# A post-norm decoder layer: V's weight fold moved beside the first unit's scores, projection biases on VectorE, first transposes of the feed-forward moved into the last gate

## The chip, the core and the metric

The kernel runs on one core of one Trainium2 chip. The metric is the device time in microseconds (us), the median of several executions. Everything is float32. The engines are TensorE (PE, with its weight loads PEld), VectorE (DVE), ScalarE (ACT), GpSimd (POOL) and SyncE (SP), which here only issues transfers. Each engine works through its own instructions in order.

## The reference, cut to what matters

```python
# x: (4, 1024, 512); every product in float32
q = (x @ wq_w + wq_b) @ vq_w.T + vq_b      # likewise k, v
# 32 channels of 16: q, k, v -> (32, 4, 1024, 16)
attn = softmax(q @ k.T / 4); o = attn @ v  # o is then reshaped and mixed
x = layernorm(x + o @ wo_w.T + wo_b)
# gated step: a convolution of two taps along the features, 4 gates
it, ot, gt, ft = split(ctx + conv(x) + bias)
ct = sigmoid(ft) * z0c + sigmoid(it) * tanh(gt); ht = sigmoid(ot) * tanh(ct)
x = layernorm(x + concat(ht, ct))
# feed-forward: x rounded to integers and scaled back, ternary weights
x = layernorm(x + dequantised(x) @ (ternary - 1).T + bias)
```

## The kernel before, in words

Two linear layers in a row are one, so the kernel first folds each pair of weights into one: `fold` (L269 to 279) multiplies `w_n` with `v_t` into `w_q`, `w_k` and `w_v`, 16 matmuls for each, in PSUM tiles that DVE and ACT copy out. The folded bias of q and k is `foldc` (L289 to 299, 16 narrow matmuls each), that of v is `foldb` (L283 to 286, 4 matmuls). SP loads the weights in the order of use; the first transfer of all is `b_o` (L60), which the output projection needs much later.

Then come 32 units of attention, a unit being 4 of the 32 channels of one batch element. `project` (L330) makes q and k of two units in pieces of 160 or 176 tokens; ACT adds the bias into `packed`, and SP scatters its rows over quadrants of 32 partitions (`to_quadrants`, L318; the tiles are named `qk`). `nat` (L390) makes the scores with queries on the partitions; DVE reduces them to the row maxima (L407), which go back into a spare row of q through DRAM (`shift`). `scores` (L444) makes the scores the other way round, ACT exponentiates them, and `weigh` (L477) multiplies with v. The loop over units (L563) starts at u = -1: this stage has only the `nat` of unit 0, 16 steps of two pairs of matmuls, and between them the pieces of `fill`: unit 2's q and the 16 pieces of `project_v` (L348), which make v of batch element 0 and which DVE evacuates, adding `b_v` (L356). From u = 0 on, the stages hold all kinds of work. Two PSUM rings are used: `ps_nat` has two tiles of two banks, `ps_st` four tiles of one bank. The order of instructions in this part, and in the tail, is the one in which the Python code issues them (`manual_schedule`).

The tail has steps: `after(n, work)` (L667) puts work n steps later, `step()` (L670) closes a step and issues what is due. A step is one gate, or one tile of the projection or of the feed-forward. For each pair of batch elements, (0, 2) and then (1, 3), there are 32 gates (`gate`, L719: three taps of 4 matmuls, two DVE additions, one ACT activation). After the fourth gate of a block `combine` (L738) forms the cell on POOL and, a step later, `second` (L745) takes the tanh on ACT. `second_norm` (L759) normalises and quantises the first two tiles ahead. Then `feed_forward` (L834) runs 16 tiles of 128 tokens. A tile is `turn` (L788: 4 transposes on TensorE, one ACT copy to `xq_t`), `feed` (L796: 4 matmuls into a ring of two PSUM tiles), `quantise` of a later tile (L779: ACT, then DVE L784 and L785), `ff_bias` (L828) and `residual` (L802: DVE L804 adds the PSUM tile, L805 takes statistics). `third_norm` (L807) normalises finished tiles and stores them, spread over later steps: aggregates on DVE (L95), a square root on ACT (L102), a reciprocal (L103) and the scaling (L111) on DVE. Between the two feed-forwards lie 16 tiles of `project_out`, whose residual input is loaded by `load_residual` a given number of steps into the first one.

Of the kernel before, what the change touches and what calls it, by code (L numbers as in the profile page):

```python
# [51 lines left out]
class Handed:  # L52
# [3 lines left out]
    def __init__(self, tc, a, shared, attn_d, eps):  # L56
        self.eps = eps
        self.nc, self.a, self.shared, self.attn_d = tc.nc, a, shared, attn_d
        self.b_o = shared.tile([P, D], F32, tag="b_o", name="b_o")
        self.nc.sync.dma_start(self.b_o, a["wo_b"].partition_broadcast(P))  # L60
        self.big, self.y, self.stats = {}, {}, {}
# [8 lines left out]
    def load_w_o(self):  # L70
        self.w_o = self.shared.tile([P, FT, D], F32, tag="w_v", name="w_o")
        self.nc.sync.dma_start(self.w_o, self.a["wo_wT"].rearrange("(t p) f -> p t f", p=P))
# [19 lines left out]
    def means(self, stats, pool, name, t0=0, n=NT):  # L92
        mv = pool.tile([P, NT, 2], F32, tag="mv", name=f"mv{name}_{t0}")
        for t in range(t0, t0 + n):
            self.nc.vector.bn_aggr(mv[:, t, :], stats[:, t, :])  # L95
        return mv

    def deviations(self, mv, pool, name, t0=0, n=NT):

        nc = self.nc  # L100
        rstd = pool.tile([P, NT], F32, tag="rstd", name=f"rstd{name}_{t0}")
        nc.scalar.activation(rstd[:, t0 : t0 + n], mv[:, t0 : t0 + n, 1], AF.Sqrt, bias=self.eps, scale=1.0)  # L102
        nc.vector.reciprocal(rstd[:, t0 : t0 + n], rstd[:, t0 : t0 + n])  # L103
        return rstd
# [87 lines left out]
def attention(ctx, tc, a, attn_d, ident, shared, hand):  # L192
# [52 lines left out]


    with tc.tile_pool(name="setup", bufs=2) as sp, tc.tile_pool(
        name="setup_ps", bufs=2, space=PSUM
    ) as ps:
        xts = {}  # L250
        for which, (w, v, dst) in enumerate((("wq", "vq", w_q), ("wk", "vk", w_k), ("wv", "vv", w_v))):
            w_n = sp.tile([P, FT, D], F32, tag="w_n", name=f"w_n{which}")
            v_t = sp.tile([P, FT, D], F32, tag="v_t", name=f"v_t{which}")
            for m in range(FT):
                rows = slice(m * P, (m + 1) * P)
                nc.sync.dma_start(w_n[:, m, :], a[f"{w}_w"][rows, :])
                nc.sync.dma_start(v_t[:, m, :], a[f"{v}_wT"][rows, :])
            w_b = sp.tile([P, FT], F32, tag="w_b", name=f"w_b{which}")
            nc.sync.dma_start(w_b, a[f"{w}_b"])
            if which < 2:  # L260
                v_b = sp.tile([P, FT], F32, tag="v_bc", name=f"v_b{which}")
                nc.sync.dma_start(v_b, a[f"{v}_bc"])
            else:
                v_b = sp.tile([P, D], F32, tag="v_b", name=f"v_b{which}")
                nc.sync.dma_start(v_b, a[f"{v}_b"].partition_broadcast(P))
            if which == 1:
                xts[0] = load_x(0)

            pts = [ps.tile([P, D], F32, tag="ps", bufs=6, name=f"fold{which}_{f}") for f in range(FT)]  # L269
            for m in range(FT):  # L270
                for f in range(FT):
                    nc.tensor.matmul(  # L272
                        pts[f], w_n[:, m, f * P : (f + 1) * P], v_t[:, m, :], start=m == 0, stop=m == FT - 1
                    )
            for f in range(FT):
                if f % 2:
                    nc.scalar.copy(dst[:, f, :], pts[f])
                else:
                    nc.vector.tensor_copy(dst[:, f, :], pts[f])
            w_bb = sp.tile([P, FT, P], F32, tag="w_bb", name=f"w_bb{which}")  # L280
            nc.vector.tensor_copy(w_bb, w_b.unsqueeze(2).to_broadcast([P, FT, P]))
            if which == 2:
                pb = ps.tile([P, D], F32, tag="ps", bufs=6, name=f"foldb{which}")  # L283
                for m in range(FT):
                    nc.tensor.matmul(pb, w_bb[:, m, :], v_t[:, m, :], start=m == 0, stop=m == FT - 1)
                nc.vector.tensor_add(b_v, pb, v_b)  # L286
                continue

            pc = ps.tile([P, FT, 32], F32, tag="pc", name=f"foldc{which}")  # L289
            for f in range(FT):  # L290
                for m in range(FT):
                    nc.tensor.matmul(
                        pc[:, f, :],
                        v_t[:, m, f * P : (f + 1) * P],
                        w_bb[:, m, 0:32],
                        start=m == 0,
                        stop=m == FT - 1,
                    )
            nc.vector.tensor_add((b_q, b_k)[which], pc[:, :, 0], v_b)

    small = ctx.enter_context(tc.tile_pool(name="asmall", bufs=2))
    packs = ctx.enter_context(tc.tile_pool(name="packs", bufs=1))
    atp = ctx.enter_context(tc.tile_pool(name="at", bufs=14))
    obuf = ctx.enter_context(tc.tile_pool(name="obuf", bufs=2))
    onp = ctx.enter_context(tc.tile_pool(name="onp", bufs=1))
    dpool = ctx.enter_context(tc.tile_pool(name="rec_d", bufs=2, space=bass.MemoryType.DRAM))
    ps_nat = ctx.enter_context(tc.tile_pool(name="ps_nat", bufs=2, space=PSUM))
    ps_st = ctx.enter_context(tc.tile_pool(name="ps_st", bufs=4, space=PSUM))
    ctx.enter_context(tc.manual_schedule())
# [20 lines left out]
    def project(p, which, t0, n, packed):  # L330

        b, gg = divmod(p, 4)
        w, bias = ((w_q, b_q), (w_k, b_k))[which]
        cols = slice(t0, t0 + n)
        pt = ps_st.tile([P, QW], F32, tag="st", name=f"proj{p}_{which}_{t0}")
        for f in range(FT):
            nc.tensor.matmul(  # L337
                pt[:, 0:n], w[:, f, gg * P : (gg + 1) * P], xts[b][:, f, cols], start=f == 0, stop=f == FT - 1
            )
        nc.scalar.activation(packed[:, cols], pt[:, 0:n], AF.Identity, bias=bias[:, gg : gg + 1], scale=1.0)  # L340
        if t0 + n == S:
            to_quadrants(2 * p, which, packed)
            if which == 0 and p > 0:
                late_rows.append(lambda: to_quadrants(2 * p + 1, 0, packed))
            else:
                to_quadrants(2 * p + 1, which, packed)

# [42 lines left out]
    def nat(u, i, pair):  # L390
# [4 lines left out]
        pt = ps_nat.tile([P, 2, 512], F32, tag="nat", name=f"nat{u}_{i}_{pair}")  # L395
        for n in range(2):
            r = 32 * (2 * pair + n)
            nc.tensor.matmul(  # L398
                pt[:, n, :],
                q_ts[u % 4][r : r + 32, qt * P : (qt + 1) * P],  # L400
                k_ts[u % 4][r : r + 32, kh * 512 : kh * 512 + 512],
                start=True,
                stop=True,
            )

        def reduce():
            nc.vector.tensor_reduce(  # L407
                mxs[u][:, qt, 2 * pair : 2 * pair + 2, kh], pt, AX.X, ALU.max, negate=True
            )
# [150 lines left out]
    for piece in qk_pieces(0, 0) + qk_pieces(0, 1):  # L560
        piece()

    for u in range(-1, NU):  # L563
# [5 lines left out]
        if u == -1:  # L569
            fill += [piece for t in range(NT) for piece in v_pieces(0, t)]  # L570
        elif units[u][0] + 1 < B:
            fill += v_pieces(units[u][0] + 1, units[u][1])
# [5 lines left out]
        if u == -1 or u + 1 == NU:  # L578
            total, done = len(fill), 0
            for i in range(HS // 2):  # L580
                if u == -1:
                    after = [nat(0, i, 0), nat(0, i, 1)]
# [22 lines left out]
        else:  # L605
# [30 lines left out]
            assert not fill  # L636
    assert not out_pieces
# [9 lines left out]
def tail(ctx, tc, a, out, ident, eps, hand):  # L647
# [71 lines left out]
    def gate(b, t, g, w):  # L719
# [4 lines left out]
        for dst, tap in ((pt[:, 0, :], 0), (pt[:, 1, :], 1), (pa, 2)):  # L724
            for i in range(FT):
# [12 lines left out]
    def combine(b, t, k):  # L738
# [17 lines left out]
        after(1, second)  # L756
        after(3, third)

    def second_norm(b, ahead=False):  # L759

        y = ys2[b]
        mv, rstd = hand.norm_stats(stats2[b], stat, f"2_{b}")

        def two(t):
            for tt in (t, t + 1):
                hand.normalised(y[:, tt, :], y[:, tt, :], mv, rstd, tt)

        two(0)
        for t in range(2, NT, 2):
            after(t // 2, lambda t=t: two(t))  # L770
        if ahead:
            quantise(b, 0)
            quantise(b, 1)

# [32 lines left out]
    def third_norm(b, t0, n, spread):  # L807
# [16 lines left out]
        after(1, deviations)  # L824
        for m in range(n // 2):
            after(2 + m, lambda ts=(t0 + 2 * m, t0 + 2 * m + 1): finish(ts))
# [7 lines left out]
    def feed_forward(batches):  # L834
# [4 lines left out]
        turn(*tiles[0])  # L839
        quantise(*tiles[2])  # L840
        for k, (b, t) in enumerate(tiles):
            if k + 1 < len(tiles):
# [27 lines left out]
    for n, batches in enumerate(((0, 2), (1, 3))):  # L870
# [9 lines left out]
        for t in range(4):  # L880
            w = w_next
            for b in batches:
                for g in range(4):
                    gate(b, t, g, w)
                    if g == 3:
                        combine(b, t, k)
# [7 lines left out]
        after(3, lambda b=batches[1]: second_norm(b))  # L894
        if n == 0:
            after(1, lambda: hand.load_attention(3, hand.shared.tile([P, NT * (D + 1)], F32, tag="big0", name="big3")))
            after(11, lambda: hand.load_residual(1))
# [45 lines left out]
```

## Time and profile before

The time is 2535.78 us, the median of 3 runs (2535.61 to 2536.34).

| | |
|---|---|
| the profiled execution, time | 2535.87 us |
| its span, first to last instruction | 2534.1 us |
| mean granted TensorE clock | 0.994 |
| PE busy | 2498.8 us (99%) |
| DVE busy | 1656.3 us (65%) |
| ACT busy | 1306.6 us (52%) |
| POOL busy | 294.2 us (12%) |
| folds and biases (span 0 to 61.66 us) | PE busy 54.09, DVE 11.75 |
| projection of units 0 and 1 (61.66 to 78.68) | PE busy 14.13 of 17.02 |
| stage u = -1 (78.68 to 142.67) | PE busy 63.95, DVE 44.05, clock 0.95 |
| attention (142.67 to 1976.00) | PE busy 1832.85 of 1833.33 |
| first feed-forward (2161.2 to 2233.1) | PE busy 65.85, DVE 59.11, clock 0.95 |
| second feed-forward to the end (2453.8 to 2534.1) | PE busy 66.48, DVE 63.11, clock 0.93 |

A matmul in float32 is recorded as two instructions, so 16 matmuls appear as x32. The start of each record tells when the array took it. Its duration[...] overlaps the next one, so costs are read from the distance between starts. An engine counts as busy also where a group of instructions contains short waits. Numbers in square brackets are idle time before an instruction and what ended it.

### The profile page before, as it was taken

The page shows a single profiled execution, that of the slowest core. Times are in us where ns is not written, and L with a number is a line of the kernel's source. Part 1 is how long each engine was busy: PE and PEld are TensorE (multiplying, and loading weights), DVE is VectorE, ACT ScalarE, POOL GpSimd, SP SyncE. Part 2 cuts the span into 40 slices and gives each one's busy share as a digit, 9 for nine tenths or more (in the row PEclk, how much of TensorE's full clock was granted, in tenths as well). Part 3 has the DMA queues.
Part 4 walks back from the last instruction along what each step waited for, and adds up shares of the span by engine and source line. Part 5 has one row for each costly group of instructions (what it writes and reads, how often), then busy time and mean ns, then how long its engine had stood idle before and what let it go on. Part 6 is the DMA issues. An engine that isn't in the chain of part 4 may idle for free.

```text
span 2534.1 us, 58831 instructions
## 1 busy us (share of the span) xinstructions
PE 2498.8 (99%) x24976; PEld 1772.6 (70%) x24976; DVE 1656.3 (65%) x2037; ACT 1306.6 (52%) x2554; POOL 294.2 (12%) x228
## 2 busy tenths in 40 slices
PE   8999999999999999999999999999999999999998
PEld 4667777777777777777777777777766688448874
DVE  1577776777777777767677777777775433875348
ACT  0146666666666666666666666666656311301122
POOL 2000000000000000000000002000021245102430
PEclk9999999999999999999999999999999999999999
DMA  4200111111111111101111114011201323231201
GB/s 141 55 13 17 24 20 53 20 24 21 20 24 23 36 39 25 21 20 21 24 20 23 21 24 128 16 24 20 76 21 49 113 102 115 83 133 49 101 17 67
DMA packets 78390, 116.77 MB, mean 46 GB/s; under 512 B 38720, under 2 KB 38720, under 8 KB 78128
## 3 DMA queue, kind: packets, MB, share of 16 engines
q1 hardware_dynamic: 77600, 111.97, 15.8%
q8 instruction: 196, 3.21, 0.5%
q0 software_dynamic: 528, 1.05, 0.1%
q14 instruction: 66, 0.54, 0.1%
HBM read 76.84 MB, written 18.35 MB: 38 GB/s over the span
## 4 chain that ended last, share of the span: by engine, by line
PE 94%; DVE 4%; ACT 1%; DMA 0%; issue 0%; POOL 0%; SPq 0%; DVEq 0%; POOLq 0%
PE nat L398 22%; PE av L487 19%; PE st L461 18%; PE proj L337 10%; PE pc L726 9%; PE v L353 5%; PE po L181 5%; PE pa L726 4%; PE fold L272 2%; PE pf L799 1%; DVE y L804 1%; DVE stats L805 1%; DVE y L111 1%; DVE y L830 1%; DVE xq L785 0%
## 5 line engine op out<-in xcount | busy, mean ns | idle before, releaser
L407 DVE TENSOR_REDUCE mx<-nat 128x2 f32<-128x1024 f32 x1024 | 1205.8, 1219 | 458.0 <-PE st L461 426.2
L472 ACT ACTIVATE at<-st 128x512 f32<-128x512 f32 x2016 | 1042.6, 602 | 613.0 <-PE st L461 609.1
L398 PE MATMUL nat<-qk 32*128 32x512 f32 x4096 | 1020.1, 615 | 3.4 <-DMA qk<-packed 2.9
L461 PE MATMUL st<-qk 32*128 32x256 f32 x8064 | 999.0, 387 | 0.0
L461 PEld LDWEIGHTS st<-qk 32*128 32x128 f32 x8064 | 656.4, 184 | 46.3 <-issue 3.6
L487 PE MATMUL av<-at,v_sb 128*32 128x256 f32 x8192 | 497.4, 382 | 0.6 <-ACT at L472 0.6
L398 PEld LDWEIGHTS nat<-qk 32*128 32x128 f32 x4096 | 346.8, 184 | 176.6 <-DVE mx L407 121.0
L487 PEld LDWEIGHTS av<-at,v_sb 128*32 128x32 f32 x8192 | 241.4, 109 | 221.6 <-ACT at L472 90.2
L534 POOL TENSOR_TENSOR o_n<-o_sb,rbc 128x512 f32<-128x512 f32 x64 | 95.0, 1507 | 1706.9 <-DMA rbc<-rec_d 1320.5
L337 PE MATMUL proj<-xT,w_qk 128*128 128x176 f32 (+1 forms) x1536 | 271.7, 321 | 0.9 <-DVE b_v L286 0.9
L337 PEld LDWEIGHTS proj<-xT,w_qk 128*128 128x128 f32 x1536 | 224.8, 190 | 66.4 <-ACT at L472 60.0
L726 PE MATMUL pc<-xf,w 128*128 128x256 f32 x1024 | 233.2, 381 | 3.2 <-DVE u L728 3.2
L726 PEld LDWEIGHTS pc<-xf,w 128*128 128x128 f32 x1024 | 195.6, 191 | 31.4 <-DVE u L728 3.6
L730 ACT ACTIVATE u<-u,b_c 128x512 f32<-128x512 f32 x64 | 46.2, 722 | 211.2 <-DVE u L729 211.2
L728 DVE TENSOR_TENSOR u<-pc,u 128x512 f32<-128x512 f32 x64 | 44.2, 691 | 142.4 <-PE pc L726 133.3
L799 PE MATMUL pf<-w_f,xq_t 128*128 128x512 f32 x256 | 121.6, 620 | 12.1 <-ACT xq_t L793 10.7
L353 PE MATMUL v<-w_v,xT 128*128 128x256 f32 x512 | 126.3, 391 | 0.0
L726 PE MATMUL pa<-xf,w 128*128 128x256 f32 x512 | 121.0, 379 | 0.0
L181 PE MATMUL po<-w_o,big 128*128 128x256 f32 (+1 forms) x360 | 117.5, 477 | 0.6 <-DVE o_sb L500 0.6
L353 PEld LDWEIGHTS v<-w_v,xT 128*128 128x128 f32 x512 | 92.4, 189 | 35.1 <-ACT at L472 16.6
L500 DVE TENSOR_TENSOR o_sb<-av,o_sb 128x256 f32<-128x256 f32 x128 | 54.3, 425 | 91.6 <-PE av L487 91.6
L726 PEld LDWEIGHTS pa<-xf,w 128*128 128x128 f32 x512 | 97.3, 190 | 13.2
(85 smaller groups left out, 1060.9 us busy)
## 6 DMA issues: line engine op xcount, KB each, us to landing
qk<-packed SPq DMA_DIRECT2D x256, 64.0 KB
w<-in_conv_wT SPq DMA_DIRECT2D x32, 512.0 KB
u<-in_ctx SPq DMA_DIRECT2D x16, 1024.0 KB
xT<-in_xT SPq DMA_DIRECT2D x16, 512.0 KB
rbc<-rec_d SPq DMA_DIRECT2D x128, 64.0 KB
attn<-o_n SPq DMA_DIRECT2D x256, 32.0 KB
big<-attn SPq DMA_DIRECT2D x4, 2048.0 KB
y<-in_x SPq DMA_DIRECT2D x4, 2048.0 KB
```

The lines of the kernel that those rows point to most:

```text
L181: nc.tensor.matmul(pt, attn_t[:, f, t * P : (t + 1) * P], self.w_o[:, f, cols], start=f == 0, stop=f == FT - 1)
L337: nc.tensor.matmul(pt[:, 0:n], w[:, f, gg * P : (gg + 1) * P], xts[b][:, f, cols], start=f == 0, stop=f == FT - 1)
L353: nc.tensor.matmul(pt, xts[b][:, f, t * P : (t + 1) * P], w_v[:, f, cols], start=f == 0, stop=f == FT - 1)
L398: nc.tensor.matmul(pt[:, n, :], q_ts[u % 4][r : r + 32, qt * P : (qt + 1) * P], k_ts[u % 4][r : r + 32, kh * 512 : kh * 512 + 512], start= ...
L407: nc.vector.tensor_reduce(mxs[u][:, qt, 2 * pair : 2 * pair + 2, kh], pt, AX.X, ALU.max, negate=True)
L461: nc.tensor.matmul(st[:, k * QW : k * QW + QW], k_ts[u % 4][r : r + 32, kt * P : (kt + 1) * P], q_ts[u % 4][r : r + 32, qq * QW : qq * QW ...
L472: nc.scalar.activation(at, st, AF.Exp, scale=0.25)
L487: nc.tensor.matmul(av[32 * j : 32 * j + 32, :], v_sb[b % 2][:, kt, c * VW : c * VW + 32], ats[u, 2 * i + n // 2, j][:, n % 2 * QW : n % 2 ...
L500: nc.vector.tensor_add(o, av, o)
L534: nc.gpsimd.tensor_mul(o_n[:, :, half * 256 : half * 256 + 256], o_sb[:, cols].rearrange("p (s e) -> p e s", e=2), rbc[:, cols].rearrange( ...
L726: nc.tensor.matmul(dst, w[:, i, tap, o : o + P], xf[:, tap, i, :], start=i == 0, stop=i == FT - 1)
L799: nc.tensor.matmul(pt, xq_ts[b, t][:, f, :], hand.w_f[:, f, :], start=f == 0, stop=f == FT - 1)
```

## The change

- **Start.** `b_o` is loaded at unit 24 with `w_o`. `v_t` of the first fold is loaded from ACT's queue, beside `w_n` from SP's. Ten matmuls of zeros, 128 x 128, are issued on TensorE ahead of the first fold.
- **Biases.** `foldc` and `foldb` are gone. DVE multiplies the rows of v's weight (1 MB more to load for each of q, k and v) with the broadcast bias, 128 x 2048, reduces to 128 x 4 and adds. V's bias goes through DRAM to a row on all partitions, by two transfers on POOL's queue.
- **V's fold.** It is cut into eight half pieces (`fold_v`, 4 matmuls 128 x 256 each, copied by ACT). Five are issued after the projections of units 0 and 1, three are the first pieces of stage u = -1.
- **Stage u = -1.** The second pair of each `nat` step now uses two one-bank tiles of `ps_st`, each with a reduction of its own (128 x 512); the first pair keeps `ps_nat`.
- **Feed-forward.** The first two tiles are turned inside the last gate, between its first and second tap. The last block's tanh (`second`) and statistics come one step later, so do the second normalisation of the second batch element and every spread third normalisation; in `second_norm` and `third_norm` the square root comes a step after the aggregates. `load_residual(1)` moves from step 11 to 13. The pools of `mv` and `rstd` get a third buffer.

```diff
     def load_w_o(self):
+        self.b_o = self.shared.tile([P, D], F32, tag="b_o", name="b_o")
+        self.nc.sync.dma_start(self.b_o, self.a["wo_b"].partition_broadcast(P))
...
+    idle = sp.tile([P, P], F32, tag="idle", bufs=1, name="idle")
+    nc.vector.memset(idle, 0.0)
+    pt = ps.tile([P, P], F32, tag="ps", name="idle_ps")
+    for n in range(10):
+        nc.tensor.matmul(pt, idle, idle, start=True, stop=True)
...
+            (nc.scalar if which == 0 else nc.sync).dma_start(v_t[:, m, :], a[f"{v}_wT"][rows, :])
...
+            nc.sync.dma_start(v_n, a[f"{v}_w"].rearrange("(t p) m -> p t m", p=P))
+            nc.sync.dma_start(w_b, a[f"{w}_b"].partition_broadcast(P))
+            nc.sync.dma_start(v_b, a[f"{v}_bc"])
+            nc.vector.tensor_mul(v_n, v_n, w_b.unsqueeze(1).to_broadcast([P, FT, D]))
+            nc.vector.tensor_reduce(dst, v_n, AX.X, ALU.add)
+            nc.vector.tensor_add(dst, dst, v_b)
...
+            nc.gpsimd.dma_start(b_d.rearrange("(t p) -> p t", p=P), dst)
+            nc.gpsimd.dma_start(b_v, b_d.partition_broadcast(P))
...
+    def fold_v(f, half):
+        cols = slice(half * QW, half * QW + QW)
+        pt = ps_st.tile([P, QW], F32, tag="st", name=f"fold2_{f}_{half}")
+        for m in range(FT):
+            nc.tensor.matmul(
+                pt, w_n[:, m, f * P : (f + 1) * P], v_t[:, m, cols], start=m == 0, stop=m == FT - 1
+            )
+        nc.scalar.copy(w_v[:, f, cols], pt)
...
-    for piece in qk_pieces(0, 0) + qk_pieces(0, 1):
+    for piece in qk_pieces(0, 0) + qk_pieces(0, 1) + folds[:5]:
...
-                    after = [nat(0, i, 0), nat(0, i, 1)]
+                    after = [nat(0, i, 0), nat(0, i, 1, apart=True)]
...
         for dst, tap in ((pt[:, 0, :], 0), (pt[:, 1, :], 1), (pa, 2)):
+            if tap == 1 and between:
+                between()
...
-        after(1, second)
-        after(3, third)
+        after(2 if last else 1, second)
+        after(4 if last else 3, third)
...
-        after(1, deviations)
+        after(2, deviations)
         for m in range(n // 2):
-            after(2 + m, lambda ts=(t0 + 2 * m, t0 + 2 * m + 1): finish(ts))
+            after(3 + m, lambda ts=(t0 + 2 * m, t0 + 2 * m + 1): finish(ts))
...
-            if k + 1 < len(tiles):
+            if 0 < k < len(tiles) - 1:
                 turn(*tiles[k + 1])
...
-                    gate(b, t, g, w)
+                    last = (b, t, g) == (batches[1], 3, 3)
+                    gate(b, t, g, w, (lambda: [turn(batches[0], tt) for tt in (0, 1)]) if last else None)
...
-        after(3, lambda b=batches[1]: second_norm(b))
+        after(4, lambda b=batches[1]: second_norm(b, False))
```

## The prediction, made before the changed kernel ran

> **What bounds the kernel now.** I read the chain that ended last first, then TensorE's timeline of the start, its granted clock in windows of 2 us, and the timelines of PE, ACT and DVE at the feed-forward.
>
> ```profile
> PE 94%; DVE 4%; ACT 1%; DMA 0%; issue 0%; POOL 0%; SPq 0%; DVEq 0%; POOLq 0%
> ```
>
> The end is TensorE's own work nearly everywhere: between 142.67 and 1976.00 us it is busy 1832.85 of 1833.33 us, and the change leaves that stretch alone. So a gain is work taken off PE, or its idle and half-clock time, in the first 142.67 us and in the two feed-forwards.
>
> ```profile
> 6.70 16.04 PE L272 MATMUL fold<-v_t,w_n 128*128 128x512 f32 x32 [6.70 <-DMA v_t<-in_vq_wT]
> 22.58 3.65 PE L292 MATMUL foldc<-w_bb,v_t 128*128 128x32 f32 x32
> 26.07 13.98 PE L272 MATMUL fold<-v_t,w_n 128*128 128x512 f32 x32
> ...
> 57.19 3.60 PE L285 MATMUL foldb<-v_t,w_bb 128*128 128x512 f32 x8
> 61.66 14.13 PE L337 MATMUL proj<-xT,w_qk 128*128 128x176 f32 x96 [0.88 <-DVE b_v L286]
> 78.68 3.90 PE L398 MATMUL nat<-qk 32*128 32x512 f32 x8 [2.88 <-DMA qk<-packed]
> ```
>
> Start, duration, group. The first fold takes 15.88 us from start to next start, the second 13.82: 2.06 us are lost at half clock, for its first weight loads are 0.85 us apart until 10.99 us and 0.43 after. Ahead of the first scores PE waits 2.88 us for rows of k.
>
> ```profile
> 80.00:82.00 2.00, 2.00 (x7) 0.87 (x4) 0.60 (x1) 0.00 (x0) 0.00 (x0) 0.50 0.67 109
> ...
> 86.00:88.00 2.00, 2.00 (x17) 1.20 (x9) 1.28 (x2) 0.00 (x0) 0.00 (x0) 1.00 0.95 354
> ```
>
> The third number from the right is the granted clock: after that wait it is one half, in finer windows from 79.2 to 86.0 us.
>
> ```profile
> 2161.23 1.04 PE L791 MATMUL tr<-ident,xq 128*128 128x128 f32 x8
> 2166.75 6.05 PE L799 MATMUL pf<-w_f,xq_t 128*128 128x512 f32 x8 [4.48 <-ACT xq_t L793]
> 2172.63 0.60 PE L791 MATMUL tr<-ident,xq 128*128 128x128 f32 x4
> ```
>
> ```profile
> 2165.59 0.63 ACT L746 ACTIVATE u<-u 128x512 f32<-128x512 f32 x1 [2.71 <-POOL u L743]
> 2166.13 0.57 ACT L793 COPY xq_t<-tr 128x512 f32<-128x512 f32 x1
> ```
>
> ```profile
> 2167.44 0.97 DVE L784 TENSOR_SCALAR xq<-xq 128x512 f32<-128x512 f32 x1 [4.41 <-ACT xq L783]
> 2168.45 1.37 DVE L785 TENSOR_SCALAR xq<-xq,sc 128x512 f32<-128x512 f32 x1
> 2169.75 0.41 DVE L784 TENSOR_SCALAR xq<-xq 128x512 f32<-128x512 f32 x1
> 2170.20 0.49 DVE L785 TENSOR_SCALAR xq<-xq,sc 128x512 f32<-128x512 f32 x1
> ```
>
> The first feed waits 4.48 us for ACT's copy, which stands behind a tanh that waits for POOL; then it runs at half clock (5.88 us to the next transposes, 3.43 when warm). The second feed-forward does the same from 2453.80 us. Once it runs, DVE is the tighter engine: a tile is 3.87 us on PE, and DVE ends each feed-forward after PE.
>
> **The start, step by step.** The sum is made against the profiled execution, 2535.87 us (span 2534.1 and 1.77 around it), 0.09 above the median 2535.78.
>
> First transfers: `b_o` (256 KB) goes away and the first pair is issued by two queues. Full-rate traffic is some 370 GB/s, so 256 KB is 0.7 us. Bounds: 1.4 us earlier (also the two late issues gone), or 0.5 later if eight transfers now share the engines and all land late; I take 0.7, fold at 6.0 us. ACT's four issues (0.43 us each) delay nothing: its first copy is due near 18 us.
>
> Clock: ten zero matmuls are 20 records of 128 columns; at half clock a 512-column record is 0.85 us, so 0.21 each, 4.3 us, from about 1.1 to 5.4. The trace's first warming took 4.3 us (6.70 to 10.99). Bounds: all of 2.06 saved, or nothing; I take 2.06, since the fold follows on their heels.
>
> Folds of q and k: 2 x 13.82 us gives 33.6; `foldc` (twice 3.49 us, 22.58 to 26.07 and the like) is gone. A wait for the last copy stays (0.88 before, I keep 0.9): projections from 34.5, and 13.97 us later, at 48.5, V's fold. DVE's new work is 3 x (2.2 + 2.2) us, estimated from 1.22 us for 1024 elements of a reduction; DVE is busy 11.75 of the first 61.66 us, so it is hidden. The rows of `vq_w` and the broadcast bias, 1.25 MB on SP ahead of k's weights, cost 3.4 us of transfer: k's are complete at about 1.6 + 5.25 MB/0.37 = 16 us, needed from 19.8; `xT` at 22, needed at 34.5; v's bias is loaded near 35 and multiplied by 40, while ACT's first copy into the same tile is due at 50. Without that cover a MB is 2.7 us. POOL's two transfers: the nearest row is `w_f` on that queue, 5.8 us to landing; two in a row end near 55, and the first user on DVE is v's first piece near 80.
>
> Five half pieces are 8 records of 256 columns; v's pieces, of that shape, start 1.72 us apart: 8.6 us, and 0.2 to begin, so the scores start at 57.3. Rows of k landed 3.0 us after the projections' end; now they land about 52. So the 2.88 us wait is covered by the fold.
>
> Here the Trainium skill, "TensorE: Matmul & The Clock Gate", section "What's actually happening", speaks against a further gain: the clock falls only after an idle window of about 3.4 us, so a wait of 2.88 would cost 2.88. The row shows the half clock from 79.2 to 86.0 after it; by the row the wait cost up to 3.4 us more. I take the row.
>
> Stage u = -1: pure work before was 16 x 1.07 (four `nat` matmuls) + 16 x 1.72 (v) + 6.8 (projection) + 16 x 0.21 (changes of kind) = 54.8 us; it took 64.0. So 9.2 us were lost, 3.4 by the clock and 5.8 in `nat` waiting for DVE to free `ps_nat`. Now three pieces (5.2) and a change (0.2) are added: 60.2. DVE has 16 x (1.15 + 2 x 0.62) + 16 x 0.42 = 45 us, so PE is the bound if the ring lets it. In the ring of four, a step's second one-bank tile waits for the reduction of one four places back; on steps with one piece that is the step before, reduced some 2.7 us after the step's start, and asked for at about 3.3 (projection) or 3.8. Behind a waiting `nat` on PE stand the pieces. Bounds: no wait, or 0.3 us each step; I take 1 us in all. The stage ends at 118.5 instead of 142.67: 24.2 us gained.
>
> **The feed-forward.** Before, from gate end 2161.23 to the second feed at 2173.07, 11.84 us hold 4.7 of work. After: the eight transposes (0.86 us) stand after the last gate's first tap, at 2157.78. Tiles 0 and 1 are quantised at 2156.79 and 2157.65, so PE does not wait, but the margin is 0.1 us. The two taps, DVE's additions and the sigmoid behind them are 0.86 later. ACT copies near 2160, ahead of that sigmoid; the first feed starts at 2162.1, warm. Next late is tile 2: sigmoid until 2163.7, ACT's rounding until 2164.6, then L784 and L785 beside POOL's products (2163.8 to 2170): slow, 0.97 + 1.37. Its transposes come at 2167.1, 1.5 us after the first feed; a 0.69 us wait at 2201 left the clock full, and I assume so here. Tile 3 costs the same 2.34 on DVE, then the bias 0.79: DVE's first L804 is at 2170.1, before 2172.84: 2.7 us. The same skill's page "SBUF — State Buffer", section "Who interferes with whom", is harsher: a two-port VectorE operation and a GpSimd one block each other for whole instructions. Each of the four would then cost up to 1.27 + 0.45 us, 6.9 instead of 4.7, and the gain be 0.5. The row decides.
>
> From there on DVE's chain sets the pace. Its waits for ACT's square roots before, 0.37 + 0.58 + 0.36 + 1.01 + 0.37 + 1.01 = 3.7 us, go, since the root is a step old when needed; quantising tile 8 right behind its normalisation adds some 0.5. So DVE gains 2.7 + 3.2 = 5.9 us, and PE, held by the ring of two until the tenth tile, 5.8 at the handover to the projections. `load_residual(1)` can start when batch 0's stores have landed, near 2215, and took about 8 us; the projection needs it near 2229. In the second feed-forward L804 comes at 2462.65 instead of 2465.89: 3.2 + 3.2 = 6.4 us at the end. Bounds for each: 3 and 8 us.
>
> Sum: 24.2 + 5.8 + 6.4 = 36.4; 2535.87 - 36.4 = 2499.5 us.
>
> **Rivals.** (a) The start stays cold, or the weights land late: zeros end half a us before the fold, and the activity window may fall badly; against it stands the near continuity. Up to 2.06 + 1.2 us lost: 2502.8. (b) DVE keeps the feed-forward: the slow quantising is worse, or waits return; each gives 3 instead of about 6: 2505.6. (c) Slower than before: in stage u = -1 each step waits for all of its own reductions, 1.22 + 2 x 0.65 = 2.5 us on DVE, with PE then falling to half clock as at 79.2. Sixteen such waits are 40 us and half clock over 60 us of work another 60: 2599. It decides from 2.6 us a step (41.5 us), which alone would end above 2541; against it, the longest wait of a step was 1.1 us, with the shallower ring, at full clock. (d) The fold pieces do not cover the rows of k, because SP sends all 16 row transfers in order: then 2.9 + 3.4 us return, 2505.8; against it, eight rows are out before k's projection ends.
>
> **How the numbers follow.** The forecast holds with 0.68 (own range 2495 to 2503), (a) 0.11, (b) 0.14, (d) 0.04, (c) 0.03. The predicted time is the likeliest, 2499.5. The range 2494 to 2508 takes in (a), (b) and (d), and below the forecast earlier weights (0.7), no ring waits (1) and both feed-forwards at 8 us (3.8). A difference of 0.2%, 5.1 us, is about what a measurement tells from no change. Every case but (c) is faster by more: faster 0.97, same 0.01, slower 0.02 ((c) with fewer waits would fall within).
>
> **What would show it.** Right: the first fold's weight loads 0.43 us apart from the start; projections at 34.5, first `nat` at 57.3 with no DMA wait and clock 1.00, first `st` at 118.5; feeds starting right at the gate's end, a wait near 1.5 us before the third pair of transposes, no ACT wait at L103. Wrong: weight loads 0.85 apart, clock below 1 in stage u = -1, PE waiting for L433 on many steps, or L784 and L785 above 1.4 us.

## The result and the profile after

| | before | after |
|---|---|---|
| time, median of 4 runs | 2535.73 us (2535.61 to 2536.34) | 2500.85 us (2499.28 to 2502.97) |
| ratio, 95% interval | | 0.9863 [0.9845, 0.9880] |
| profiled execution: time, span, clock | 2535.87, 2534.1, 0.994 | 2499.28, 2497.5, 0.999 |

The forecast was 2499.5 us, range 2494 to 2508. The profiled execution fell on it almost exactly, but one term of its gain came by chance, as will be seen: its span fell by 36.6 us, the median by 34.9.

The shares of the chain that ended last are still TensorE's:

```profile
PE 94%; DVE 5%; DMA 0%; issue 0%; ACT 0%; SPq 0%; POOL 0%; DVEq 0%; POOLq 0%
```

TensorE's timeline of the start, after (start, duration, group):

```profile
1.05 4.48 PE L269 MATMUL idle_ps<-idle 128*128 128x128 f32 x20 [1.05 <-DVE idle L266]
5.36 27.63 PE L307 MATMUL fold<-v_t,w_n 128*128 128x512 f32 x64
33.67 14.16 PE L346 MATMUL proj<-xT,w_qk 128*128 128x176 f32 x96 [0.68 <-ACT w_qk L312]
47.67 8.80 PE L361 MATMUL fold<-v_t,w_n 128*128 128x256 f32 x40
56.40 1.12 PE L421 MATMUL nat<-qk 32*128 32x512 f32 x3
57.27 0.66 PE L421 MATMUL nats<-qk 32*128 32x512 f32 x1
57.32 0.59 PE L421 MATMUL nat<-qk 32*128 32x512 f32 x1
57.70 1.09 PE L421 MATMUL nats<-qk 32*128 32x512 f32 x3
```

Folds in one piece, no 2.88 us wait ahead of the scores. The last four lines are one group of eight records, though, with the next work at 58.72: 2.32 us where 1.07 is the work. The wait for rows of k is not all gone; 1.25 us of it hides between the records.

TensorE's and then VectorE's timeline at the first feed-forward, after:

```profile
2131.82 1.04 PE L836 MATMUL tr<-ident,xq 128*128 128x128 f32 x8
2140.99 0.63 PE L836 MATMUL tr<-ident,xq 128*128 128x128 f32 x4 [1.24 <-DVE xq L830]
2146.32 3.67 PE L844 MATMUL pf<-w_f,xq_t 128*128 128x512 f32 x8 [0.83 <-DVE y L849]
```

```profile
2138.53 0.90 DVE L829 TENSOR_SCALAR xq<-xq 128x512 f32<-128x512 f32 x1 [0.58 <-ACT xq L828]
2139.47 1.37 DVE L830 TENSOR_SCALAR xq<-xq,sc 128x512 f32<-128x512 f32 x1
2140.76 1.51 DVE L829 TENSOR_SCALAR xq<-xq 128x512 f32<-128x512 f32 x1
2142.30 1.37 DVE L830 TENSOR_SCALAR xq<-xq,sc 128x512 f32<-128x512 f32 x1
2143.60 1.77 DVE L875 TENSOR_TENSOR y<-y,b_f 128x512 f32<-128x512 f32 x1
2145.48 0.69 DVE L849 TENSOR_TENSOR y<-pf,y 128x512 f32<-128x512 f32 x1
```

The first feed no longer waits, and TensorE's waits are now for VectorE. VectorE's first addition of a PSUM tile (L849, before L804) comes 15.39 us after the last gate's start. Before, it came 16.79 us after it:

```profile
2172.84 0.69 DVE L804 TENSOR_TENSOR y<-pf,y 128x512 f32<-128x512 f32 x1 [1.55 <-PE pf L799]
```

Five VectorE instructions in a row are slow, the bias L875 among them (0.69 us elsewhere), all while GpSimd's five products run:

```profile
2137.87 1.28 POOL L781 TENSOR_TENSOR u<-u,big 128x512 f32<-128x512 f32 x1 [2.68 <-ACT u L769]
2139.23 1.32 POOL L782 TENSOR_TENSOR u<-u 128x512 f32<-128x512 f32 x1
2140.63 1.35 POOL L786 TENSOR_TENSOR y<-u,big 128x512 f32<-128x512 f32 x1
2141.95 1.44 POOL L787 TENSOR_TENSOR u<-u 128x512 f32<-128x512 f32 x1
2143.47 1.35 POOL L788 TENSOR_TENSOR y<-u,big 128x512 f32<-128x512 f32 x1
```

The two engines go in step: each of the four roundings (L829, L830) ends 0.28 or 0.29 us behind the end of one product, and the bias 0.55 behind the end of the fifth. So one VectorE instruction goes by with each product.

**Where the 36.6 us come from.** Stage u = -1 ended at 142.67 and ends at 118.98, just ahead of the first `st` matmul (the scores with keys on the partitions): 23.69. The attention stretch from there to the gates: 0.21. The handover from the output projection to the gates: 2.06. The first feed-forward, from the last gate's start to the projections, took 77.06 and takes 71.88: 5.18. The second, from the last gate's start to the end, 85.48 and 80.01: 5.47. The lines for the first `st`, the last gate and the first projection, before and then after:

```profile
142.69 0.70 PE L461 MATMUL st<-qk 32*128 32x256 f32 x4
2156.05 3.62 PE L726 MATMUL pc<-xf,w 128*128 128x256 f32 x16
2233.11 17.33 PE L181 MATMUL po<-w_o,big 128*128 128x512 f32 x40
```

```profile
118.99 0.70 PE L491 MATMUL st<-qk 32*128 32x256 f32 x4
2130.09 1.89 PE L765 MATMUL pc<-xf,w 128*128 128x256 f32 x8
2201.97 13.47 PE L185 MATMUL po<-w_o,big 128*128 128x512 f32 x31
```

The handover is the term that came by chance. It is one wait of TensorE's timeline, before and after:

```profile
2004.04 5.41 PE L726 MATMUL pc<-xf,w 128*128 128x256 f32 x16 [3.23 <-DVE u L728]
```

```profile
1979.77 3.72 PE L765 MATMUL pc<-xf,w 128*128 128x256 f32 x16 [2.86 <-DVE u L767]
```

VectorE waits there for the gates' input (7.9 us for `u<-in_ctx`), which no edit touches. Before, half clock followed (5.41 instead of 3.72 us); here it did not, and run e1 below tells why.

### The profile page after: what moved, and what is told of

Its sections match the earlier page's. It is cut to its first block, busy times and chain, and to the rows that moved or that the text cites. A ratio compares the mean times of both kernels' runs of the same rounds, so it can differ in the third digit from the quotient of the medians.

```text
span 2497.5 us, 58830 instructions
## 1 busy us (share of the span) xinstructions
PE 2476.3 (99%) x24956; PEld 1766.8 (71%) x24956; DVE 1670.5 (67%) x2055; ACT 1309.9 (52%) x2560; POOL 293.5 (12%) x230
## 4 chain that ended last, share of the span: by engine, by line
PE 94%; DVE 5%; DMA 0%; issue 0%; ACT 0%; SPq 0%; POOL 0%; DVEq 0%; POOLq 0%
PE nat L421 21%; PE av L517 19%; PE st L491 18%; PE proj L346 10%; PE pc L765 9%; PE v L371 5%; PE pa L765 4%; PE po L185 4%; PE fold L307 1%; PE pf L844 1%; DVE y L849 1%; DVE y L875 1%; DVE y L115 1%; DVE stats L850 1%; DVE xq L830 1%; PE fold L361 1%
## 5 line engine op out<-in xcount | busy, mean ns | idle before, releaser
L437 DVE TENSOR_REDUCE mx<-nat 128x2 f32<-128x1024 f32 x1008 | 1187.5, 1219 | 453.8 <-PE st L491 424.2
L844 PE MATMUL pf<-w_f,xq_t 128*128 128x512 f32 x256 | 115.6, 595 | 4.5 <-DVE y L849 3.0
```

What stands on the lines that cost most here:

```text
L437: nc.vector.tensor_reduce(mxs[u][:, qt, 2 * pair : 2 * pair + 2, kh], pt, AX.X, ALU.max, negate=True)
L844: nc.tensor.matmul(pt, xq_ts[b, t][:, f, :], hand.w_f[:, f, :], start=f == 0, stop=f == FT - 1)
```

## The experiments

Every run is compared with its own runs of the kernel before. What an undone part costs in the feed-forwards is read from the profiles, by the two stretches just named (FF1, FF2), since the times of one kernel spread over 1.5 to 4 us. In the profiles of the change, e1, e2, e3, e9 and e11, whose feed-forwards are the same, these stretches agree within 0.2 us, but for one FF1 (e9) that is 0.4 longer.

| run | time, us | ratio, 95% interval | FF1 | FF2 |
|---|---|---|---|---|
| the change | 2500.85 | 0.9863 [0.9845, 0.9880] | 71.88 | 80.01 |
| e1 the same again | 2500.84 | 0.9863 [0.9848, 0.9877] | | |
| e2 no zeros | 2501.68 | 0.9864 [0.9847, 0.9880] | | |
| e3 fold first | 2507.15 | 0.9888 [0.9874, 0.9903] | | |
| e4 start only | 2512.94 | 0.9909 [0.9894, 0.9923] | 77.19 | 85.90 |
| e5 turns at the start | 2499.66 | 0.9865 [0.9850, 0.9880] | 71.02 | 79.17 |
| e6 tanh at its old step | 2505.08 | 0.9889 [0.9873, 0.9906] | 74.65 | 82.78 |
| e7 roots with aggregates | 2508.15 | 0.9898 [0.9883, 0.9913] | 75.12 | 83.36 |
| e8 bias of two tiles early | 2496.98 | 0.9854 [0.9840, 0.9869] | 69.43 | 77.59 |
| e9 one ring | 2506.24 | 0.9880 [0.9865, 0.9895] | | |
| e10 bias and tile 2 early | 2497.86 | 0.9848 [0.9834, 0.9863] | 69.79 | 77.94 |
| e11 V's bias later | 2500.33 | 0.9858 [0.9842, 0.9875] | | |
| e12 e8 and e11 | 2493.52 | 0.9836 [0.9822, 0.9849] | 69.45 | 77.46 |

**e1, the changed kernel again.**

> The changed kernel once more, unaltered. Its first four times were 2499.28, 2499.67, 2502.97 and 2502.02 us, and its profile showed no half clock anywhere, while the kernel before lost about 2.3 us at the handover to the gates (a 3.23 us wait and half clock after it; now 2.86 us at full clock). Theory A: whether a wait of about 2.9 us ends in half clock is a matter of where it falls, so the times come in groups near 2499.5 and 2502.5, and a profile of the slower group shows half clock after one of the waits (near 1980 or 56 us). Theory B: the spread is of the transfers at the start, the clock is full in both groups, and only the time of the first fold differs.

This profile, span 2499.7, has the half clock, from 1980.29 to 1983.70, after the same wait (2.91 us). Over all 14 profiles of this study the wait lasted 2.54 to 3.23 us; in seven half clock followed (after 2.54, 2.61, 2.63, 2.79, 2.91, 2.96, 3.23), in seven not (2.79, 2.83, 2.83, 2.86, 3.02, 3.14, 3.17). So its length does not decide.

Its place does. In the clock records of the 14 traces every half-clock stretch ahead of the kernel's end lasts 3.41 or 6.83 us, and every full-clock stretch between two changes is a whole multiple of 3.41 us. The clock is thus set in windows of 3.41 us, whose edges can be counted forward from any change. Two windows of the change and then two of e1, cut at these edges (TensorE's busy time follows the comma, the clock is third from the right):

```profile
1974.73:1978.14 3.41, 2.17 (x11) 1.56 (x9) 0.00 (x0) 0.00 (x0) 0.00 (x0) 1.00 0.86 301
1978.14:1981.56 3.42, 1.79 (x8) 1.62 (x9) 2.44 (x5) 0.99 (x1) 0.00 (x0) 1.00 1.06 406
```

```profile
1976.88:1980.29 3.41, 0.50 (x4) 0.10 (x2) 0.69 (x1) 0.00 (x0) 0.00 (x0) 1.00 1.05 404
1980.29:1983.71 3.42, 3.42 (x8) 2.79 (x9) 3.31 (x7) 2.39 (x3) 0.00 (x0) 0.50 1.04 407
```

In the change the wait lies across an edge, 1.2 us in one window and 1.6 in the next, and the clock stays full. In e1 all 2.9 us lie in one window, and the next one has half clock. Over the 14 traces half clock followed each of the 15 full-clock windows in which TensorE was idle for 2.15 us or more, and none in which it was idle for 1.99 us or less. (Two more falls, in e9 and e10, came after 2.1 us of waiting in pieces between overlapping records, which can't be measured so closely.) Where the edges fall differs between executions of one kernel, so the 2 us of the handover are luck.

Theory A holds for the mechanism, 1.7 us of the spread; the start of the first fold, 4.76 to 5.48 us in profiles with the zeros, adds 0.7. The grouping of the four times is not fully explained by these.

**e2, without the zeros:** the ten `idle` matmuls and their memset are deleted.

> The change without its ten matmuls of zeros; the rest is unaltered. Theory A (the prediction's): the first fold starts at 5.4 us as before but takes 15.9 us instead of 13.8 from start to start, and the time is 2.1 us above the changed kernel's. Theory B: the loads of k's weights or rows are late anyway, and the 2.1 us are waited for elsewhere: less than 0.7 us.

TensorE's timeline:

```profile
4.38 29.38 PE L302 MATMUL fold<-v_t,w_n 128*128 128x512 f32 x64 [4.38 <-DMA v_t<-in_vq_wT]
34.44 14.16 PE L341 MATMUL proj<-xT,w_qk 128*128 128x176 f32 x96 [0.68 <-ACT w_qk L307]
...
57.16 0.70 PE L416 MATMUL nat<-qk 32*128 32x512 f32 x2
57.18 0.70 PE L416 MATMUL nats<-qk 32*128 32x512 f32 x2
57.70 0.59 PE L416 MATMUL nat<-qk 32*128 32x512 f32 x2
57.71 0.59 PE L416 MATMUL nats<-qk 32*128 32x512 f32 x2
58.24 1.99 PE L356 MATMUL fold<-v_t,w_n 128*128 128x256 f32 x8
```

Cold, the folds take 1.75 us more. But they start when the weights land, at 4.38; with the zeros they start when these end, 0.4 to 1.1 us later. The projections gain 0.8 to 1.4 us by the zeros, and the rows of k take that back: the group after the first scores starts at 58.24 here, and at 56.93 to 59.55 in the nine profiles with the zeros and the same start. Theory B: nothing that can be measured.

**e3, V's fold first.**

```diff
-    for piece in qk_pieces(0, 0) + qk_pieces(0, 1) + folds[:5]:
+    for piece in folds[:5] + qk_pieces(0, 0) + qk_pieces(0, 1):
```

> The five half pieces of V's fold are issued ahead of the projections of units 0 and 1 instead of behind them; nothing else differs. PE then has nothing between the last projection and the first scores, as in the kernel before. Theory A (the row of before): a wait for rows of k near 2.9 us returns, half clock follows for several us, and since 1.0 us of wait is there now, the time rises by 1.9 us of wait and up to 3.4 us of clock: 5.3 in all. Theory B (the rule that the clock falls only after a longer idle window): the wait comes back at full clock, and the time rises by 1.9 us.

TensorE's timeline, then windows:

```profile
59.63 2.27 PE L421 MATMUL nat<-qk 32*128 32x512 f32 x4 [2.87 <-DMA qk<-packed]
60.90 2.71 PE L421 MATMUL nats<-qk 32*128 32x512 f32 x4
63.54 3.78 PE L361 MATMUL fold<-v_t,w_n 128*128 128x256 f32 x8
```

```profile
62.00:64.00 2.00, 2.00 (x5) 0.49 (x3) 1.99 (x3) 0.00 (x0) 0.00 (x0) 0.50 0.67 150
64.00:66.00 2.00, 2.00 (x6) 1.55 (x6) 0.42 (x1) 0.00 (x0) 0.00 (x0) 0.50 1.03 383
```

The wait of before is back (2.88 then, 2.87 now) with half clock behind it until 67; eight fold records take 3.71 us to the next start instead of 1.93. The first `st` comes at 125.60, 6.6 us later than in the change, and the time is 6.3 us above the change's median. Theory A, the row of before, and more than its 5.3; what makes up the rest is open. Full clock after the wait would have given 1.9.

**e4, the start alone:** turns, tanh, roots and residual load as before.

> The change with its tail undone: turns, tanh, roots and the residual load stand where they stood before. Theory A: the first scores of the other kind start at 119.0 us, 23.7 earlier than before, and the time is 23.7 below the kernel before, 2512.0, for the handover's 2.3 us come from the clock's phase and not from an edit. Theory B: the handover's 2.3 us belong to the start's edits, for instance to the output bias that is loaded later: 2509.8. Theory C: the three gains aren't additive, and the feed-forward alone gives less than 10 us of the rest.

The first `st` is at 118.96, 23.7 earlier than before, the handover has the half clock (wait 2.96), and FF1 and FF2 are those of before within 0.5 us. The time is 22.6 us below its own runs of before (2535.53), 12.1 above the change. Theory A: the parts add up, and the handover's 2 us belong to no edit.

**e5, e6, e7, one part of the tail undone in each.**

```diff
e5
-                    gate(b, t, g, w, (lambda: [turn(batches[0], tt) for tt in (0, 1)]) if last else None)
+                    gate(b, t, g, w)
...
+        turn(*tiles[0])
         quantise(*tiles[2])
e6
-        after(2 if last else 1, second)
-        after(4 if last else 3, third)
+        after(1, second)
+        after(3, third)
e7
-        after(2, deviations)
+        after(1, deviations)
```

> The change with one part undone: tiles 0 and 1 of each feed-forward are turned at its start again, not within the last gate; tanh and roots stay a step later. Theory A (the start of the feed-forward is set by VectorE, whose rounding of tiles 2 and 3 begins after the last sigmoid either way): TensorE waits about 2 us more for ScalarE's copies, but VectorE's first addition of a PSUM tile moves by less than 1 us, and the time rises by at most 1 us for each feed-forward, 2 in all. Theory B (the prediction's picture that the first feed's 4.5 us and half clock were a loss of their own): 3 us each, 6 in all.

> The change with one part undone: the last block's tanh, its statistics and the second batch element's second normalisation come at the steps of before; the turns stay in the last gate and the roots a step later. Theory A: ScalarE's rounding of tile 2 stands behind the tanh, which waits for GpSimd's products, so VectorE's first addition comes 2.5 us later than in the change, and the time rises by 2.5 for each feed-forward, 5 in all. Theory B: the roundings then fall outside GpSimd's products and run at 0.42 and 0.49 us instead of 0.90 to 1.51, which gives back 2.4 us of it: 1 us or less in all.

> The change with one part undone: the square roots of the second and third normalisations stand in the step of their aggregates again, and the residual load at step 11; turns and tanh stay as changed. Theory A (the prediction): VectorE waits 3.2 to 3.7 us for ScalarE's roots in each feed-forward and these are on the path: 6.4 to 7 us in all. Theory B: VectorE's waits are taken up by slack of the two PSUM tiles, and less than half of it is seen: under 3.5 us.

*e5.* Theory A allowed a rise of up to 1 us each; with the turns back at the start the feed-forwards are shorter, by 0.86 and 0.84 us: just the 0.86 by which eight transposes within the last gate delay its sigmoid. The first feed waits 1.14 us for ScalarE's copy, which costs nothing, for VectorE's first addition is later still. So theory A's reason holds, and the turn within the gate even costs a little. The times can't tell the two kernels apart (ratio 0.9865 against 0.9863).

*e6.* 2.77 us more in each, 5.5 in all, the size of theory A, but in another place than it said. TensorE's timeline:

```profile
2143.26 1.09 PE L836 MATMUL tr<-ident,xq 128*128 128x128 f32 x4 [5.14 <-DVE xq L830]
2144.14 5.36 PE L844 MATMUL pf<-w_f,xq_t 128*128 128x512 f32 x8
2149.34 0.60 PE L836 MATMUL tr<-ident,xq 128*128 128x128 f32 x4
```

The transposes of the third tile wait 5.14 us instead of 1.24, half clock follows (5.20 instead of 3.44 us for the feed), and from there TensorE runs without a wait: it is the bound, while VectorE's first addition is only 0.8 us later: GpSimd's last product ends at 2142.82, and the second tile's rounding (0.41 and 0.49 us) and the bias (0.69) behind it are quick again (theory B's reason).

*e7.* 3.24 and 3.35 us more: theory A. Two waits carry it, on TensorE's timeline at feeds 5 and 9, counted from 0, whose tiles VectorE rounds behind its waits for the roots:

```profile
2161.79 3.70 PE L844 MATMUL pf<-w_f,xq_t 128*128 128x512 f32 x8 [1.58 <-ACT xq_t L838]
...
2180.18 3.70 PE L844 MATMUL pf<-w_f,xq_t 128*128 128x512 f32 x8 [1.50 <-ACT xq_t L838]
```

Undone one at a time they give -1.7 + 5.5 + 6.6 = 10.4 us; the change has 10.65.

**e8, bias of two tiles early:** `ff_bias(b, 0)` and `ff_bias(b, 1)` behind `quantise(b, 1)` in `second_norm`, and in the feed-forward only for k > 1.

> The change with one move more: the feed-forward bias of tiles 0 and 1 is added ahead of the feed-forward, right behind their rounding in the gates, instead of one step each in front of the first two additions of a PSUM tile (1.75 and 0.69 us of VectorE). Theory A (VectorE sets the pace of the feed-forward's start): its first addition comes 1.8 us earlier, the following ones 2.4, and the time falls by about 2 for each feed-forward, 4 in all. Theory B (TensorE is the next bound, as its waits are then for ScalarE's copies and VectorE's roundings): at most 1 us each.

2.45 and 2.42 us less: theory A. The addition stands right behind the roundings, and with one input in PSUM it is not slowed, although GpSimd's last product runs beside it (2145.28 to 2146.64):

```profile
2144.11 1.38 DVE L832 TENSOR_SCALAR xq<-xq,sc 128x512 f32<-128x512 f32 x1
2145.41 0.68 DVE L851 TENSOR_TENSOR y<-pf,y 128x512 f32<-128x512 f32 x1
```

**e9, one ring:** `apart=True` is left out.

> The change with one part undone: in stage u = -1 both pairs of a score step use the ring of two two-bank tiles again, with one reduction of 1024 elements each. Theory A (the prediction): the stalls of before, 5.8 us there, return, less the 1 us or so that the change has: the time rises by 4.8 us. Theory B: with three more pieces of other work in the stage VectorE has time to catch up, and half or less returns: 2.5 us.

The rows of k came late in this run (2.1 us of waiting in the first scores), and half clock followed for 3.4 us, in e10's start too. From the first work behind the first scores to the first `st` it is 65.02 us here, 61.92 in e10, alike but for the ring, so the ring is worth 3.1 us: between the two theories. The 5.4 us by which the time rises contain the late rows and the half clock.

**e10, bias and tile 2 early:** as e8, and `quantise(b, 2)` behind `two(2)` in the gates.

> The change with more moved ahead of the feed-forward: the bias of tiles 0 and 1 as in the run before (which gave 3.7 us), and tile 2 is rounded behind its normalisation in the gates, before GpSimd's last products begin. Theory A: the wait before the third pair of transposes (1.2 to 1.5 us) goes, VectorE does at most one slow rounding before its first addition of a PSUM tile, and the time falls by 2 x 1.4 us more than in that run, 6.5 below the change. Theory B: the waits come back as waits of TensorE for VectorE some tiles later, as VectorE's chain is only begun sooner: the same as that run, 3.7 below the change.

Theory B: no more than e8. The wait for the third transposes is gone, but GpSimd's products now meet other VectorE work, the scaling of two tiles (1.0 us in the change):

```profile
2145.61 2.86 DVE L115 TENSOR_SCALAR y<-y,mv,rstd 128x512 f32<-128x512 f32 x2
```

**e11 and e12, V's bias later:** both transfers move to SP, behind the last piece ahead of stage u = -1; e12 adds e8's move.

```diff
-            nc.gpsimd.dma_start(b_d.rearrange("(t p) -> p t", p=P), dst)
-            nc.gpsimd.dma_start(b_v, b_d.partition_broadcast(P))
...
+    nc.sync.dma_start(b_d.rearrange("(t p) -> p t", p=P), b_vc)
+    nc.sync.dma_start(b_v, b_d.partition_broadcast(P))
```

> The change with V's bias sent later: its two transfers (512 pieces of 4 bytes to DRAM, then 256 KB back) are issued by SP behind the rows of q and k instead of by GpSimd beside them. Theory A: the small pieces hold up the rows of k (14.0 us for 16 issues in the first profile, 11.84 before); now the issues take 12 us or less in every run, the first group of scores takes 1.1 us instead of 2.3, and the time falls by 1.2 us. Theory B: the rows are paced by SP's own 0.59 us an issue, and nothing changes but what a measurement can't tell: less than 0.5 us.

> The two moves that the runs before favour, together in the changed kernel: the bias of tiles 0 and 1 ahead of each feed-forward (3.7 us below the change when alone), and V's bias sent by SP behind the rows of k (its profile's first scores did not wait, but its time could not be told from the change's). Theory A: both are on the path and add up, since one lies in the start and the other in the feed-forwards: 3.7 + 1.2 = 4.9 us below the change, near 2496. Theory B: the rows of k wait for nothing that this moves, and the time is that of the bias alone, near 2497.

SP issues the 16 rows of q and k over 14.0 us in the change and over 12.5 in e11 and e12. In these two the first scores take 1.07 us and wait for nothing, and the first `st` comes at 118.20 and 117.83. But in the profiles with GpSimd's transfers the rows took 11.9 to 14.9 us, twice with no wait either (e2, e6), so that these transfers hold up the rows is likely and not shown. e11's time can't be told from the change's. e12 is 2493.52 us, ratio 0.9836 against 0.9863, 7.3 us below the change: more than theory A's 4.9. Profile against profile, both with full clock at the handover, it is 4.92 us, which is theory A; the rest lies within the spread of the change's own times. It is the best of all.

## Why the prediction was right, and where it was not

- **Start, 24.2 predicted, 23.69.** *Transfers and folds:* fold at 5.36 (6.0), projections at 33.67 (34.5), scores at 56.40 (57.3), each better by under a us. *Cold clock, 2.06:* the cost is 1.75, but the zeros' own length and the rows of k leave nothing of it that can be measured (e2). As a gain of the edit the term is wrong: the weights were there at 4.38 (e2), and the zeros held the fold back to 5.36.
- **Wait for rows of k:** "the 2.88 us wait is covered by the fold" held but for 1.25 us. The rows were assumed to land about 52; SP issued the last at 54.8. **Half clock after it:** the row of before was the right guide, e3 shows it. The Trainium skill, "TensorE: Matmul & The Clock Gate", section "What's actually happening", gives about 3.4 us of idle window for the fall; it also says there that the window runs freely. The traces agree on a free window of 3.41 us (e1), but it need not be idle throughout: 2.15 us were enough, and the 2.88 us of before lay in one window.
- **Stage u = -1, 61.2:** 62.6, of which 1.25 is the wait above. The ring gave 3.1 us (e9), not 5.8 - 1 = 4.8: part of the loss of before would have gone with the added pieces alone. Rival (c), a wait at each step, did not occur: TensorE waited 1.0 us for L437 in the whole run.
- **Feed-forward, 5.8 and 6.4:** 5.18 and 5.47. The step that was mis-sized is "DVE's first L804 is at 2170.1, before 2172.84: 2.7 us" (3.2 in the second): by the distance from the last gate's start it came 1.4 and 1.9 us sooner. The four roundings took 5.15 us instead of 4.7 (one of them 1.51, above the 1.4 that the prediction named as a sign of being wrong), and the bias behind them 1.77 instead of 0.79, for GpSimd was not done. The skill's page "SBUF — State Buffer", section "Who interferes with whom", names that case, a VectorE instruction with two SBUF inputs beside a reading GpSimd; I had weighed its rule for the roundings only. For these, 5.15 lies between the row's 4.7 and the rule's 6.9: the engines do wait for each other, but one rounding went by with each product, about 1.4 us from product to product, and not 1.27 + 0.45. The rest of the gain, 3.8 and 3.6 us, came in VectorE's chain behind the first addition, near the 3.7 - 0.5 of the prediction; e7 puts 3.2 and 3.4 of it down to the roots.
- **The turns:** the prediction counted the first feed's 4.48 us and half clock among the losses, and had the turn repair it. TensorE did lose that time, but nothing was gained by it: VectorE's chain was the bound, and the turn delays it (e5). Moving the tanh was what counted, 5.5 us (e6).
- **Sum:** too high by 0.5, 0.6 and 0.9 us, and too low by 2.3 that nobody forecast. The median is 1.4 above the forecast; e1 suggests that some of its runs had the half clock.

## What to carry to other kernels

Before an engine's wait is repaired, ask which engine's chain ends the stage: TensorE's waits of 1.1 us (e5) cost nothing where VectorE was later, and 5.1 us (e6) made TensorE the bound. A cheap instruction is not cheap beside GpSimd: list every VectorE instruction in that stretch, count a GpSimd product for each that is slowed, and move the ones that can be done earlier (e8). One profile of a wait of 2.5 to 3.2 us is not enough to price the clock behind it: find the clock's windows in the trace, and see whether the wait can fall into one of them.

## What was not expected of the hardware

- Waits of 2.54 us were followed by half clock and waits of 3.17 us were not, in kernels with the same work there: what counts is the idle time within one window of 3.41 us, and the limit lay between 1.99 and 2.15 us (e1).
- Beside GpSimd's products the roundings, the bias and the scalings of VectorE were slowed (0.42 to 1.51, 0.69 to 1.77, 0.5 to 1.5 us); its addition of a PSUM tile and its statistics kept 0.68 and 0.69 us (e8).
- At the very start the clock column shows 1.00 while weight loads are 0.85 us apart (e2, 5.4 to 7.1 us): the trace's first clock record lies at 7.7 us, and the half rate before it is seen only in the spacing.
- The 2 KB of V's bias, in pieces of 4 bytes, took 7.6 to 9.2 us to land from GpSimd's queue, and the 256 KB behind it 5.1 to 7.0; 5.8 had been assumed for each.
